# Self-attention in slots of one head: TensorE's instructions in a written order, and the causal mask added by VectorE

## The chip, the cores and the metric

The kernel runs on one core of a Trainium2 chip. The metric is the device time of one execution in microseconds (us). A core has TensorE (matrix products, PE in the profile, with its weight loads as PEld), VectorE (DVE), ScalarE (ACT), GpSimd (POOL) and SyncE (SP, which here issues transfers). They run side by side and wait for each other by semaphores. TensorE writes its results into PSUM[...]; everything else lies in SBUF.

## The reference

A decoder layer on x of shape (4, 512, 512) in fp32: self-attention, then a cross-attention to a context of (4, 512, 128), then a mixture of experts. Only the first part is touched:

```python
qkv = einsum('bsh,ph->bsp', layernorm(x), weight_qkv)   # 4 groups of 4 query heads, one key, one value head
scores = einsum('bsgqd,btgd->bgqst', q, k) / sqrt(128)
scores = where(causal, scores, finfo.min)
attn = softmax(scores, axis=-1)
out = einsum('bgqst,btgd->bsgqd', attn, v).reshape(b, s, 16 * 128)
x = x + einsum('bse,he->bsh', out, weight_proj)
```

There are four sequences (b) of 512 tokens, four groups (g) of four query heads (h), 64 heads in all, each of width 128.

## The kernel before

Tokens are cut into four tiles of 128 rows (s or i), and the 512 columns of x into four parts of 128 (c). For each sequence `norm_and_v` normalises x on VectorE and GpSimd (L143 to L151), turns it by transposes on TensorE into `xnT` (L171, copied out of PSUM by ScalarE) and computes the values `v` (`pv`, L220). For each group `project` computes the keys `kT`, and for each head the queries `qT` (`pq`, L236), each four products of 128x512 accumulated in one PSUM bank and copied out by ScalarE (L245, L248).

For each head, `softmax_rows` goes over the four row tiles i. Because of causality, tile i needs only the first (i+1)*128 columns of scores. It computes `sc` in PSUM (L258), and adds the mask of the diagonal block by a second product on TensorE, `ident16` times `mask16` in bf16, into the same bank (L265). VectorE takes the negated row maximum (L268), ScalarE the exponential with the row sum (L271), and VectorE divides (L279, L282). `attend` transposes the 10 blocks of the probabilities `pr` on TensorE (`tp`, L290), copies them to `prT` (L294; the copy for i = 1 by ScalarE, the others by VectorE), multiplies with `v` into `po` (L297), and ScalarE copies that to `oT` (L305). `add_projection` (L312, L319) multiplies the four `oT` of a group by `wpr`, and VectorE adds the result to x. For the last sequence these products (`pl` there) are done later, as filling in the cross-attention.

The softmax of a head is written ahead of `attend` of the head before it (`late`). No order is pinned in this part: the framework's scheduler takes the instructions by their priority and by its own estimate of what is ready, and fixes the order in which they stand on each engine. From the cross-attention on, the order is that of the program (`tc.keep_in_program_order`, through the wrapper `Ordered`).

PSUM is shared by tags with two banks each: `mm` (values, queries, keys, output products), `sc`, `t` (transposes) and `po`. `pr` has two buffers, `prT` one, `qT` three.

Of the kernel before, what the change touches and what calls it, by code (L numbers as in the profile page):

```python
# [35 lines left out]
def decoder_kernel(  # L36
# [23 lines left out]
    ident16 = const.tile([P, P], BF16, tag="ident16", name="ident16")  # L60
    nc.vector.tensor_copy(ident16, ident)
    maskf = const.tile([P, P], F32, tag="maskf", name="maskf")
    make_causal_mask(nc, maskf, mask_val=MASK)
    mask16 = const.tile([P, P], BF16, tag="mask16", name="mask16")
    nc.vector.tensor_copy(mask16, maskf)
# [68 lines left out]

    xb = [xpool.tile([P, NT, HID], F32, tag=f"x{b}", name=f"x{b}") for b in range(B)]
# [26 lines left out]
    def layernorm(b, dst):  # L162

        for part in norm_parts(b, dst, nc.vector, nc.gpsimd, nc.vector):
            part()

    def transpose_in(ps, src, dst, s, copy, bufs=2):

        t = ps.tile([P, NC, P], F32, tag="t", name="t", bufs=bufs)
        for c in range(NC):  # L170
            nc.tensor.transpose(t[:, c, :], src[:, c * P : (c + 1) * P], ident)  # L171
        copy(dst[:, :, s * P : (s + 1) * P], t)

# [5 lines left out]
    with ExitStack() as ph:  # L179
# [4 lines left out]
        nc.sync.dma_start(xb[0], x[0].rearrange("(s p) d -> p s d", p=P))  # L184
        wqkv_v = wqkvT.rearrange("(c p) (g w) -> p c g w", p=P, g=NKV)
        wv = wp.tile([P, NC, NKV, D], F32, tag="wv", name="wv")
        for c in range(NC):
            nc.sync.dma_start(wv[:, c], wqkv_v[:, c, :, (QPG + 1) * D :])
        wqk, wpr = [], []
        for g in range(NKV):  # L190
            t = wp.tile([P, NC, (QPG + 1) * D], F32, tag=f"wqk{g}", name=f"wqk{g}")
            nc.sync.dma_start(t, wqkv_v[:, :, g, : (QPG + 1) * D])
            wqk.append(t)
            t = pj.tile([P, QPG, HID], F32, tag=f"wpr{g}", name=f"wpr{g}")
            nc.sync.dma_start(
                t,
                wprojT[g * QPG * D : (g + 1) * QPG * D].rearrange(
                    "(h p) d -> p h d", p=P
                ),
            )  # L200
            wpr.append(t)
            if g + 1 < B:
                nc.sync.dma_start(
                    xb[g + 1], x[g + 1].rearrange("(s p) d -> p s d", p=P)
                )

        def norm_and_v(b):
            xnT = p2.tile([P, NC, S], F32, tag="xnT", name=f"xnT{b}", bufs=1)
            xn = [
                p2.tile([P, HID], F32, tag="xn", name=f"xn{b}_{s}", bufs=4)  # L210
                for s in range(NT)
            ]
            layernorm(b, lambda s: xn[s])
            for s in range(NT):
                transpose_in(ps, xn[s], xnT, s, nc.scalar.copy)
            v = []
            for s in range(NT):
                pv = ps.tile([P, HID], F32, tag="mm", name=f"pv{b}_{s}")
                for c in range(NC):
                    nc.tensor.matmul(  # L220
                        pv,
                        lhsT=xnT[:, c, s * P : (s + 1) * P],
                        rhs=wv[:, c].rearrange("p g d -> p (g d)"),
                        start=c == 0,
                        stop=c == NC - 1,
                    )
                vt = p2.tile([P, NKV, D], F32, tag="v", name=f"v{b}_{s}", bufs=5)
                nc.scalar.copy(vt.rearrange("p g d -> p (g d)"), pv)
                v.append(vt)
            return xnT, v  # L230

        def project(b, g, h, xnT):

            pq = ps.tile([P, S], F32, tag="mm", name=f"pq{b}_{g}_{h}")
            for c in range(NC):
                nc.tensor.matmul(  # L236
                    pq,
                    lhsT=wqk[g][:, c, h * D : (h + 1) * D],
                    rhs=xnT[:, c, :],
                    start=c == 0,  # L240
                    stop=c == NC - 1,
                )
            if h == QPG:
                t = p2.tile([P, S], F32, tag="kT", name=f"kT{b}_{g}")
                nc.scalar.copy(t, pq)  # L245
            else:
                t = p2.tile([P, S], F32, tag="qT", name=f"qT{b}_{g}_{h}", bufs=3)
                nc.scalar.mul(t, pq, QSCALE)  # L248
            return t

        def softmax_rows(b, g, h, qT, kT):
# [3 lines left out]
            for i in range(NT):  # L255
                n = (i + 1) * P
                sc = ps.tile([P, S], F32, tag="sc", name=f"sc{b}_{g}_{h}_{i}")
                nc.tensor.matmul(  # L258
                    sc[:, :n],
                    lhsT=qT[:, i * P : n],  # L260
                    rhs=kT[:, :n],
                    start=True,
                    stop=False,
                )
                nc.tensor.matmul(  # L265
                    sc[:, i * P : n], lhsT=ident16, rhs=mask16, start=False, stop=True
                )
                nc.vector.tensor_reduce(  # L268
                    nmx[:, i : i + 1], sc[:, :n], AX.X, ALU.max, negate=True
                )  # L270
                nc.scalar.activation(  # L271
                    pr[:, OFF[i] : OFF[i] + n],
                    sc[:, :n],
                    AF.Exp,
                    bias=nmx[:, i : i + 1],
                    accum_out=sm[:, i : i + 1],
                )
            rs = small.tile([P, NT], F32, tag="rs", name=f"rs{b}_{g}_{h}")
            nc.vector.reciprocal(rs, sm)  # L279
            for i in range(NT):  # L280
                q = pr[:, OFF[i] : OFF[i] + (i + 1) * P]
                nc.vector.tensor_scalar(q, q, rs[:, i : i + 1], None, ALU.mult)  # L282
            return pr

        def attend(b, g, h, pr, v):
            prT = p2.tile([P, NT, S], F32, tag="prT", name=f"prT{b}_{g}_{h}", bufs=1)
            for i in range(NT):
                t = ps.tile([P, NC, P], F32, tag="t", name=f"tp{b}_{g}_{h}_{i}")
                for j in range(i + 1):
                    nc.tensor.transpose(  # L290
# [4 lines left out]
            po = ps.tile([P, S], F32, tag="po", name=f"po{b}_{g}_{h}")  # L295
            for j in range(NT):
                nc.tensor.matmul(  # L297
                    po[:, j * P :],
                    lhsT=v[j][:, g, :],
                    rhs=prT[:, j, j * P :],  # L300
                    start=j == 0,
                    stop=j == NT - 1,
                )
            o = pj.tile([P, S], F32, tag="oT", name=f"oT{b}_{g}_{h}", bufs=NKV * QPG)
            nc.scalar.copy(o, po)  # L305
            return o

        def add_projection(b, g, outs):
            for s in range(NT):
                pj = ps.tile([P, HID], F32, tag="mm", name=f"pj{b}_{g}_{s}")  # L310
                for h in range(QPG):
                    nc.tensor.matmul(  # L312
                        pj,
                        lhsT=outs[h][:, s * P : (s + 1) * P],
                        rhs=wpr[g][:, h, :],
                        start=h == 0,
                        stop=h == QPG - 1,
                    )
                nc.vector.tensor_tensor(xb[b][:, s, :], pj, xb[b][:, s, :], ALU.add)  # L319

        late = None
        last_outs = []

        def finish(b, g, h, pr, v, outs):
            outs.append(attend(b, g, h, pr, v))
            if h == QPG - 1:
                if b == B - 1:
                    last_outs.append(outs)
                else:
                    add_projection(b, g, outs)  # L330

        for b in range(B):
            xnT, v = norm_and_v(b)
            for g in range(NKV):
                kT = project(b, g, QPG, xnT)
                outs = []
                for h in range(QPG):
                    qT = project(b, g, h, xnT)
                    pr = softmax_rows(b, g, h, qT, kT)
                    if late is not None:  # L340
                        finish(*late)
                    late = (b, g, h, pr, v, outs)
        finish(*late)


# [6 lines left out]


    pinned = False

    class Ordered:
        def __init__(self, engine):
            self.engine = engine

        def __getattr__(self, name):  # L360
            def call(*args, **kw):
                i = getattr(self.engine, name)(*args, **kw)  # L362
                if pinned:
                    tc.keep_in_program_order(i)
                return i

            return call

    tensor, vector, scalar, gpsimd, sync = (
        Ordered(e) for e in (nc.tensor, nc.vector, nc.scalar, nc.gpsimd, nc.sync)  # L370
    )
# [108 lines left out]
    with ExitStack() as ph:  # L480
# [415 lines left out]
        pinned = False  # L896
# [189 lines left out]
    with ExitStack() as ph:  # L1086
# [71 lines left out]
        pinned = True  # L1158
# [22 lines left out]
        pinned = False  # L1181
# [48 lines left out]
```

## Time and profile before

| | us |
|---|---|
| median of three runs | 2058.51 (2058.48 to 2058.69) |
| the profiled execution | 2059.55 |
| its span | 2057.7 |
| self-attention, to the first `pl` on TensorE | 908.91 |
| cross-attention and experts, the rest of the span | 1148.8 |

A row of a timeline gives the start and the length in us, the engine, the line, the operation, output<-input, and in brackets how long the engine had sat idle before it and for what. A row of a group gives the count, then the busy time in us and the mean of one in ns, then the idle time before them. A row of the busy time per stretch gives the stretch, its length, and for PE, PEld, DVE, ACT and POOL the busy us with the number of instructions in brackets, then the granted clock of TensorE, the share of the transfer engines and GB/s. An fp32 product stands in the profile as two passes (two rows), a transpose or a bf16 product as one. The recorded length of a pass is longer than the distance to the next one, as passes overlap.

### The profile page before, as it was taken

Reading aid. Unit: us, or ns where it says so; the run is one execution under the profiler, and the core shown is the slowest. Engines: PE = TensorE matmul, PEld = TensorE weight load, DVE = VectorE, ACT = ScalarE, POOL = GpSimd, SP = SyncE. Lnnn points to the kernel's source line nnn. Section 1 sums busy time; section 2 is a strip of 40 time slices with the busy share of each in tenths; the row PEclk is TensorE's granted clock in tenths of the full one; section 3 lists DMA queues with packets and bytes.
Section 4 is the critical chain, followed back from the end, with each engine's and each line's share of the span. In section 5 each row is a group of like instructions: output and inputs, shape, how many; then the busy total and the mean of one; then the engine's idle time right before and its main releaser. Section 6 shows DMA issues by size and latency. Waiting matters only on the chain. (4 is left out here: it accounts for less than half of the span.)

```text
span 2057.7 us, 22666 instructions
## 1 busy us (share of the span) xinstructions
PE 2020.7 (98%) x8507; PEld 946.0 (46%) x8507; DVE 867.4 (42%) x1843; ACT 680.0 (33%) x1479; POOL 197.8 (10%) x182
## 2 busy tenths in 40 slices
PE   7999999999999999999999999999999999999997
PEld 3555555554555545552233333333333354655664
DVE  4334344332444334435666656565656261111111
ACT  2322332222333224332555444444444201222221
POOL 1000000000000000010022020220200000233331
PEclk9999999999999999999999999999999999999999
DMA  8000000000000000000002300100010084333331
GB/s 286 0 1 0 1 0 0 1 0 0 1 0 1 0 1 0 1 25 19 17 14 51 86 12 17 52 13 12 21 49 6 1 286 136 76 62 59 67 56 22
DMA packets 52508, 74.80 MB, mean 36 GB/s; under 512 B 9889, under 2 KB 27809, under 8 KB 52402
## 3 DMA queue, kind: packets, MB, share of 16 engines
q1 hardware_dynamic: 43666, 54.73, 8.7%
q0 software_dynamic: 8736, 18.62, 5.0%
q8 instruction: 70, 1.15, 0.2%
q14 instruction: 36, 0.29, 0.0%
HBM read 47.60 MB, written 18.61 MB: 32 GB/s over the span
## 5 line engine op out<-in xcount | busy, mean ns | idle before, releaser
L362 DVE TENSOR_REDUCE cnmx<-s 128x1 f32<-128x512 f32 x512 | 329.2, 685 | 199.5 <-PE s L362 199.3
L362 ACT ACTIVATE w<-s 128x512 f32<-128x512 f32 x512 | 277.9, 594 | 338.9 <-PE s L362 338.8
L362 PE MATMUL s<-ckT,cqT 32*128 32x512 f32 x1024 | 308.8, 641 | 1.0 <-DVE cnmx L362 1.0
L236 PE MATMUL pq<-xnT,wqk 128*128 128x512 f32 x640 | 300.9, 593 | 0.0
L362 PE MATMUL s<-cqT,ckT 32*128 32x512 f32 x1024 | 294.8, 640 | 0.0
L268 DVE TENSOR_REDUCE nmx<-sc 128x1 f32<-128x128 f32 (+3 forms) x256 | 125.7, 491 | 185.0 <-PE sc L265 184.8
L271 ACT ACTIVATE pr<-sc,nmx 128x128 f32<-128x128 f32 (+3 forms) x256 | 135.1, 528 | 155.9 <-DVE nmx L268 155.9
L294 DVE COPY prT<-tp 128x128 f32<-128x128 f32 (+2 forms) x192 | 97.0, 507 | 206.4 <-PE tp L290 206.3
L258 PE MATMUL sc<-kT,qT 128*128 128x128 f32 (+3 forms) x512 | 181.3, 463 | 0.0
L312 PE MATMUL pj<-wpr,oT 128*128 128x512 f32 x384 | 171.8, 595 | 0.0
L362 PE MATMUL sh<-fnT,sw 128*128 128x512 f32 x320 | 154.0, 612 | 0.0
L297 PE MATMUL po<-prT,v 128*128 128x512 f32 (+3 forms) x512 | 149.4, 434 | 4.3 <-DVE prT L294 4.3
L236 PEld LDWEIGHTS pq<-xnT,wqk 128*128 128x128 f32 x640 | 110.6, 191 | 85.6 <-issue 85.5
L362 PEld LDWEIGHTS s<-cqT,ckT 32*128 32x128 f32 x1024 | 80.5, 183 | 145.3 <-ACT w L362 108.7
L362 PE MATMUL cpo<-w,vpad 128*32 128x512 f32 x1024 | 137.2, 608 | 0.0
L297 PEld LDWEIGHTS po<-prT,v 128*128 128x128 f32 x512 | 96.6, 190 | 84.5 <-issue 45.4
L248 ACT ACTIVATE qT<-pq 128x512 f32<-128x512 f32 x64 | 38.2, 597 | 225.0 <-PE pq L236 225.0
L362 PE MATMUL y<-w3all,hT 128*128 (+1 forms) x234 | 107.3, 594 | 3.1 <-ACT yo L1142 2.5
L258 PEld LDWEIGHTS sc<-kT,qT 128*128 128x128 f32 x512 | 81.4, 189 | 56.1 <-ACT qT L248 20.2
L312 PEld LDWEIGHTS pj<-wpr,oT 128*128 128x128 f32 x384 | 69.4, 190 | 77.4 <-issue 71.1
L290 PE MATMUL tp<-ident,pr 128*128 128x128 f32 x640 | 102.4, 275 | 1.3 <-DVE prT L294 1.3
L290 PEld LDWEIGHTS tp<-ident,pr 128*128 128x128 f32 x640 | 71.9, 141 | 62.6 <-issue 43.6
(162 smaller groups left out, 1948.7 us busy)
## 6 DMA issues: line engine op xcount, KB each, us to landing
w1all<-in_w1T SPq DMA_DIRECT2D x8, 704.0 KB
w2all<-in_w2T SPq DMA_DIRECT2D x8, 704.0 KB
wqk<-in_wqkvT SPq DMA_DIRECT2D x4, 1280.0 KB
x<-in_x SPq DMA_DIRECT2D x4, 1024.0 KB
wpr<-in_wprojT SPq DMA_DIRECT2D x4, 1024.0 KB
cqT<-cxnT SPq DMA_DIRECT2D x128, 32.0 KB
ckT<-ctxT SPq DMA_DIRECT2D x128, 32.0 KB
normed<-fxn SPq DMA_DIRECT2D x4, 1024.0 KB
```

The source lines that it names most:

```text
L236: nc.tensor.matmul(pq, lhsT=wqk[g][:, c, h * D : (h + 1) * D], rhs=xnT[:, c, :], start=c == 0, stop=c == NC - 1,)
L248: nc.scalar.mul(t, pq, QSCALE)
L258: nc.tensor.matmul(sc[:, :n], lhsT=qT[:, i * P : n], rhs=kT[:, :n], start=True, stop=False,)
L268: nc.vector.tensor_reduce(nmx[:, i : i + 1], sc[:, :n], AX.X, ALU.max, negate=True)
L271: nc.scalar.activation(pr[:, OFF[i] : OFF[i] + n], sc[:, :n], AF.Exp, bias=nmx[:, i : i + 1], accum_out=sm[:, i : i + 1],)
L290: nc.tensor.transpose(t[:, j, :], pr[:, OFF[i] + j * P : OFF[i] + (j + 1) * P], ident)
L294: copy(prT[:, : i + 1, i * P : (i + 1) * P], t[:, : i + 1, :])
L297: nc.tensor.matmul(po[:, j * P :], lhsT=v[j][:, g, :], rhs=prT[:, j, j * P :], start=j == 0, stop=j == NT - 1,)
L312: nc.tensor.matmul(pj, lhsT=outs[h][:, s * P : (s + 1) * P], rhs=wpr[g][:, h, :], start=h == 0, stop=h == QPG - 1,)
L362: i = getattr(self.engine, name)(*args, **kw)
```

## The change

The self-attention is rewritten as a list of small jobs that a loop puts in an order, and every TensorE instruction keeps that order. One turn of the loop is a slot. In it head u has its scores computed, and the head before it (`held`) its transposes and its product with the values.

- In the first half of a slot, scores 0 to 3 of head u, each followed by some projection jobs for the next head (`ahead`); in the second half, transposes 0 to 3 of the held head, each followed by jobs of `waiting`, that is output products of an earlier group or the first values; then the held head's `po`. The list `room` says how many jobs follow each step; a slot has 8 to 10 of them where there is enough waiting.
- The mask is no longer a product. VectorE adds `maskf` to the diagonal block in PSUM, ahead of its maximum. `ident16` and `mask16` go.
- At the end of a sequence the transposes of the next sequence's x stand between the scores of the last head; its values follow the last `po` of the old sequence in one block.
- The first sequence's x is loaded in four transfers in place of one, with moments, root and normalisation for each tile apart. The first group's `wqk` is issued ahead of `wv`.
- The other engines are not pinned in this part; the scheduler places their instructions around TensorE's order. In the experts' loop the pin is now for TensorE alone; only TensorE's calls go through the wrapper there in both kernels.

```diff
+    pinned_mm, pinned = True, False
...
+                if pinned or pinned_mm and self is tensor:
+                    tc.keep_in_program_order(i)
...
-        nc.sync.dma_start(xb[0], x[0].rearrange("(s p) d -> p s d", p=P))
+        for s in range(NT):
+            nc.sync.dma_start(xb[0][:, s, :], x[0, s * P : (s + 1) * P])
...
-        for c in range(NC):
-            nc.sync.dma_start(wv[:, c], wqkv_v[:, c, :, (QPG + 1) * D :])
         wqk, wpr = [], []
         for g in range(NKV):
...
             nc.sync.dma_start(t, wqkv_v[:, :, g, : (QPG + 1) * D])
             wqk.append(t)
+            if g == 0:
+                for c in range(NC):
+                    nc.sync.dma_start(wv[:, c], wqkv_v[:, c, :, (QPG + 1) * D :])
...
+        def norm_first():
...
+            for s in range(NT):
...
+                nc.vector.bn_stats(st, xb[0][:, s, :])
+                nc.vector.bn_aggr(mv, st)
...
+                nc.vector.tensor_scalar(rstd, mv[:, 1:2], EPS, None, ALU.add)
+                nc.gpsimd.tensor_tensor(rstd, rstd, mhalf[:, 0:1], ALU.pow)
+                nc.vector.tensor_scalar(
+                    xn, xb[0][:, s, :], mv[:, 0:1], rstd, ALU.subtract, ALU.mult
+                )
...
+        def product(name, operands, done):
+            held = []
+
+            def job(k, lhsT, rhs):
+                if k == 0:
+                    held.append(ps.tile([P, S], F32, tag="mm", name=name))
+                tensor.matmul(
+                    held[0], lhsT=lhsT, rhs=rhs, start=k == 0, stop=k == len(operands) - 1
+                )
+                if k == len(operands) - 1:
+                    done(held[0])
+
+            return [lambda k=k, o=o: job(k, *o) for k, o in enumerate(operands)]
...
+            def part(i):
                 n = (i + 1) * P
                 sc = ps.tile([P, S], F32, tag="sc", name=f"sc{b}_{g}_{h}_{i}")
-                nc.tensor.matmul(
...
-                nc.tensor.matmul(
-                    sc[:, i * P : n], lhsT=ident16, rhs=mask16, start=False, stop=True
-                )
+                tensor.matmul(
+                    sc[:, :n], lhsT=qT[:, i * P : n], rhs=kT[:, :n], start=True, stop=True
+                )
+                nc.vector.tensor_tensor(
+                    sc[:, i * P : n], sc[:, i * P : n], maskf, ALU.add
+                )
                 nc.vector.tensor_reduce(
...
+            def divide():
+                rs = small.tile([P, NT], F32, tag="rs", name=f"rs{b}_{g}_{h}")
+                nc.vector.reciprocal(rs, sm)
+                for j in range(NT):
+                    w = pr[:, OFF[j] : OFF[j] + (j + 1) * P]
+                    nc.vector.tensor_scalar(w, w, rs[:, j : j + 1], None, ALU.mult)
...
+        waiting, ahead, held = values(0), [], None
+        for u in units + [None]:
+            between, turns = [lambda: None] * NT, []
+            take = 4
+            if u is not None:
+                b, g, h = u
+                pr, between, divide = scores(u)
+                if (b, g) == (0, 0):
+                    take = 8 if h < 2 else 0
                 else:
...
+                    take = (4, 5, 5, 2)[h]
+                if (g, h) == (NKV - 1, 1) and b + 1 < B:
+                    norm(b + 1)
+                if h + 1 < QPG:
+                    ahead = project(b, g, h + 1)
+                elif g + 1 < NKV:
+                    ahead = project(b, g + 1, QPG) + project(b, g + 1, 0)
+                elif b + 1 < B:
+                    turns = [lambda s=s: turn(b + 1, s) for s in range(NT)]
+
+            room = [1, 1, 1, 1, 1, 1, 0, 2] if held else [1, 1, 1, 1, 0, 0, 0, 0]
+            total = min(take, len(waiting)) + len(ahead) + (8 if turns else 0)
+            for k in (1, 2, 0, 3, 7, 5, 4) * 2:
+                room[k] += sum(room) < total
+            for k in (5, 4, 0, 3, 2, 1) * 2:
+                room[k] -= sum(room) > total and room[k] > 0
+            steps = attend(*held) if held else []
+            for k in range(2 * NT):
+                if k < NT:
+                    between[k]()
+                    if turns:
+                        turns.pop(0)()
+                        if not turns:
+                            ahead = project(b + 1, 0, QPG) + project(b + 1, 0, 0)
+                elif steps:
+                    steps.pop(0)()
+                for _ in range(room[k]):
+                    some = ahead or waiting
+                    if some:
+                        some.pop(0)()
+            for job in ahead:
+                job()
+            ahead = []
+            for step in steps:
+                step()
+            if u is not None:
+                divide()
+            if held:
+                b_, g_, h_ = held[0]
+                if h_ == QPG - 1 and b_ < B - 1:
+                    waiting += output(b_, g_)
+                if h_ == QPG - 1 and g_ == NKV - 1 and b_ < B - 1:
+                    for job in values(b_ + 1):
+                        job()
+            held = (u, pr) if u is not None else None
```

`values`, `project` and `output` make their jobs with `product`; `attend` gives the four transpose steps and the step of `po`, with the same instructions as before.

## The prediction

> **What bounds the kernel now.** First the page. TensorE is busy for 98% of the span, the next engine for 42%:
>
> ```profile
> PE 2020.7 (98%) x8507; PEld 946.0 (46%) x8507; DVE 867.4 (42%) x1843; ACT 680.0 (33%) x1479; POOL 197.8 (10%) x182
> ```
>
> A busy TensorE need not run at its pace, so the stretch of the self-attention comes next, then its timeline. By the view of busy time per stretch, of the first 905 us:
>
> ```profile
> 0.00:905.00 905.00, 886.52 (x3128) 472.20 (x3128) 361.65 (x878) 278.93 (x752) 15.64 (x38) 1.00 0.05 18
> ```
>
> VectorE is busy for 40% and ScalarE for 31%: neither bounds the stage. The granted clock is 1.00. The order of the two built programs is the same, instruction for instruction, from the last head to the end, so only these 905 us can change. One head on TensorE:
>
> ```profile
> 312.24 0.38 PE L258 MATMUL sc<-kT,qT 128*128 128x128 f32 x2
> 312.46 0.22 PE L265 MATMUL sc<-mask,ident 128*128 128x128 bf16 x1
> 312.51 0.65 PE L258 MATMUL sc<-kT,qT 128*128 128x256 f32 x2
> ...
> 315.30 0.22 PE L265 MATMUL sc<-mask,ident 128*128 128x128 bf16 x1
> 315.36 0.50 PE L290 MATMUL tp<-ident,pr 128*128 128x128 f32 x3
> 315.69 1.88 PE L312 MATMUL pj<-wpr,oT 128*128 128x512 f32 x4
> 317.41 2.32 PE L297 MATMUL po<-prT,v 128*128 128x512 f32 x8
> 319.56 2.39 PE L312 MATMUL pj<-wpr,oT 128*128 128x512 f32 x5
> ```
>
> Read the starts, not the durations. Four passes of 512 columns take 317.41 - 315.69 = 1.72 us, 0.429 each (an fp32 matmul is two passes, a transpose one); the eight passes of `po` 2.15 us; a transpose 0.109 (three in 0.33). The scores have the shapes of `po`, so their floor is 2.15 too. But 312.24 to 315.69 is 3.45 us, and its scores and seven transposes are worth 2.15 + 0.76 = 2.91: 0.54 us a head goes to the masks. Of this 4 x 0.056 = 0.22 is their own time; the rest is in score passes that start late behind a mask, or behind the exp that frees their bank.
>
> The floor without masks: 640 `pq`, 384 `pj` and 128 `pv` passes at 0.429 = 494.2; 64 `po` and 64 score sets at 2.15 = 275.2; 704 transposes at 0.109 = 76.7; together 846.1 us. The masks add 256 x 0.056 = 14.3. The stage ends here:
>
> ```profile
> 905.82 2.42 PE L297 MATMUL po<-prT,v 128*128 128x512 f32 x8 [0.78 <-DVE prT L294]
> 908.91 1.55 PE L362 MATMUL pl<-wpr,oT 128*128 128x512 f32 x3 [0.68 <-ACT oT L305]
> ```
>
> 908.9 - 860.4 = 48.5 us are lost: 14.1 at the start (below), 64 x 0.32 = 20.5 around the masks, some 14 at batch changes and in the last heads.
>
> **The change part by part: the masks.** Their removal gives 14.3 + 20.5 = 34.8 us, if no other wait takes the same place. [...] The trace decides: passes follow at 0.429 us with a load of 0.19 us each hidden. A load is exposed only behind something as short as a mask, and a transpose (0.109) just covers one. I keep 34.8.
>
> VectorE gets 256 adds on PSUM. No row shows VectorE writing PSUM. Nearest rows:
>
> ```profile
> L319 DVE TENSOR_TENSOR x<-pj,x 128x512 f32<-128x512 f32 x48 | 33.2, 691 | 111.6 <-PE pj L312 111.6
> L294 DVE COPY prT<-tp 128x128 f32<-128x128 f32 x64 | 18.6, 291 | 203.8 <-PE tp L290 203.7
> ```
>
> Bounds: 0.19 us (the 128-wide cast that goes away) and 0.69 (the 512-wide sum); I take 0.29. [...] 256 x 0.29 = 74 us of VectorE against 14 of TensorE. [...] With 361.65 us busy it goes to 436 of some 890, 49%. So the add costs nothing by its sum; its place in the chain counts.
>
> **The chain in a slot.** TensorE now may not pass a waiting instruction. A slot is: scores 0 to 3 of head u with projection jobs between them (a job is two passes, 0.858 us), the transposes of head u-1 with jobs between, then `po` of u-1. By the order view VectorE does, after score 3: add, maximum, first prT copy, reciprocal, four divides, two prT copies; `po` waits for the last copy. Durations:
>
> ```profile
> 315.56 0.69 DVE L268 TENSOR_REDUCE nmx<-sc 128x1 f32<-128x512 f32 x1 [0.44 <-PE sc L265]
> 316.28 0.69 ACT L271 ACTIVATE pr<-sc,nmx 128x512 f32<-128x512 f32 x1 [0.46 <-DVE nmx L268]
> 316.87 0.19 ACT L271 ACTIVATION_READ_ACCUMULATOR pr<-sc,nmx 128x1 f32 x1
> 317.09 0.18 DVE L279 RECIPROCAL rs<-sm 128x4 f32<-128x4 f32 x1 [0.25 <-ACT pr L271]
> 317.31 1.27 DVE L282 TENSOR_SCALAR pr<-pr,rs 128x128 f32<-128x128 f32 x4
> ```
>
> From the end of score 3: 0.20 until VectorE sees it (315.36 to 315.56), add 0.29, step 0.04, maximum 0.69, exp and sum 0.81, reciprocal and divides 1.52, copies 0.47 + 0.68 (of 128x384 and 128x512, the first 0.55 by its row, 0.08 of it under its neighbour), load and start of `po` 0.15: 4.8 us. TensorE gets there after five jobs and ten transposes, 4.29 + 1.09 = 5.38. Slack 0.55, so no wait in the 30 full slots of this form; in 12 (h = 2) an x sum of 0.61 stands ahead of the copies: slack nil. Exposed waits, by kind of slot:
> - h = 3, nine slots: the eight jobs run k, then q. An output product is open in one of the two `mm` banks, so q's first job waits until ScalarE has copied kT: 0.20 + 0.59 + load 0.15 = 0.95. 8.6 us.
> - Thin slots (four jobs; group 0 and most of the last batch), ten. Exp 0 ends 0.22 + 0.20 + 0.29 + 0.04 + 0.29 + 0.03 + 0.46 = 1.53 us into the slot, with a load 1.68; score 2 is there at 0.22 + 0.43 + 0.86 = 1.51: 0.18. Transposes 2 need the first copy's bank: behind the add, 0.49 + 0.29 + 0.16 = 0.94 after score 3, and TensorE is there at 0.33: 0.61. The copies stand ahead of the divides here, so `po` does not wait. 7.9 us.
> - Three last slots of a batch: kT waits 0.95 for the fourth xnT copy, q 0.95 for kT: 5.7. Three first slots: score 2 0.18, transposes 2 (first copy behind the maximum, 1.66 against 1.18) 0.48, transposes 3 (the copy on ScalarE behind exp 3, 2.56 against 1.99) 0.57: 3.7.
> - Last head and drain, nothing between: score 2 (1.69 against 0.65) 1.04, score 3 0.19, transposes 2 0.61, `po` for the copies of transposes 3 1.04; then 0.43, 1.04, and `pl` for oT (0.20 + 0.59 + load) 0.94: 5.3.
>
> **The start.**
>
> ```profile
> 6.51 1.29 DVE L143 BATCH_NORM_STATS2 st<-x 128x6 f32<-128x512 f32 x2 [6.51 <-DMA x<-in_x]
> ...
> 11.58 2.91 PE L171 MATMUL t<-ident,xn 128*128 128x128 f32 x12 [11.58 <-DVE xn L151]
> ...
> 16.71 13.04 PE L220 MATMUL pv<-wv,xnT 128*128 128x512 f32 x30
> ...
> 29.59 0.59 PE L236 MATMUL pq<-xnT,wqk 128*128 128x512 f32 x1
> ```
>
> By 29.59 TensorE did 32 x 0.429 + 16 x 0.109 = 15.5 us: 14.1 lost. Now x[0] comes in quarters. At 391 GB/s (the rate of 10 to 40 us) 1.05 MB took until 6.51, so quarters land at some 4.5, 5.2, 5.8 and 6.5 (bounds 4.5 and 6.5 for all; the last one counts). The last moments are done at 7.4; SP's three further issues of 0.44 delay what follows by 1.3, under the transfer. GpSimd's four powers (1.0 each in place of one) end at 9.2, the last xn at 9.7, its transposes and copy at 11.3; kT starts at 11.6, 9.85 lost. wqk0 (1.31 MB more, now ahead of wv) is in at 9.9. Then sc0 waits 0.95 for qT, and sc2 0.8, since VectorE has the norm of x[1] (landing 18.8, moments 2.9, power 1.0, a multiply) queued ahead of the first add. 11.6 us in all. The two casts that go (0.19, 0.22) were hidden behind the moments. Moved projections and transposes are the same instructions, at their floor.
>
> **The sum.** Lost after: 11.6 + 8.6 + 7.9 + 5.7 + 3.7 + 5.3 = 42.8, and 1 for small bubbles as in the trace. The first `pl` comes at 846.1 + 43.8 = 889.9 in place of 908.9: 19 us sooner. The profiled execution took 2059.55 us (span 2057.7, 1.85 around it), 1.04 above the median of 2058.51; from the median, 2039.5.
>
> **The rivals.**
> *The order feeds TensorE better than I count* (kT's copy and the thin slots' waits hidden): only start and end are lost, 846.1 + 16.9 = 863, 46 us sooner: 2012.6. Against it: the bank that q needs is plainly held.
> *The wait at `po` takes the masks' place* (slower). If the chain is longer than 4.8 by d, the 12 slots lose d and the 30 lose d - 0.55. At d = 0.85 the gain is gone; at 0.95 it is slower by over 0.2%; at 1.2, 34 us lost, 2073.5. For it: a read behind a PSUM write on one engine is in no row, and an add of 0.69 is 0.40 by itself. Against: VectorE's step from reciprocal to divide is 0.04.
> *The start and the small waits eat it.* If VectorE's norms in the first slots wait on late loads (5 us) and each wait above is half again as long (16 us), 2058: no difference.
> That the order is not what the diff says is ruled out by the order view.
>
> **How the numbers follow.** My forecast (waits as counted, within some 12 us) 0.75, 2040; better feeding 0.09; `po` waits 0.11, of which 0.02 within 0.2% and 0.08 slower; start and small waits 0.05, mostly no difference. 0.2%, 4.1 us, is about what a measurement can tell. Faster 0.86, same 0.06, slower 0.08. The add at 0.69 costs 12 x 0.4 = 5 us, at 0.19 gains nothing; the start's bounds 2 us either way; the range goes from 2025, where half of the 26 us of waits in the slots are hidden, to 2055, where `po` waits as with d = 0.75.
>
> **What would show it.** The first `pl` near 890 us; no row of masks; score passes of 384 and 512 columns at 0.322 and 0.429; an L336 add at 0.29; `po` with little wait for prT; q's load waiting for kT nine times near 0.9. Wrong if `po` waits over 0.3 us in most slots, if an add takes over 0.6, or if the start is not 2 us earlier.

## The result, and the profile after

The changed kernel takes 2042.55 us (median of four runs, 2040.03 to 2043.65); the kernel before, run beside it, 2058.59. The ratio is 0.992, with a 95% interval of 0.9903 to 0.9938: faster by 0.8%. The profiled execution took 2043.63 us, its span 2041.7.

First the page's line of engines, then the view of busy time per stretch up to the end of the self-attention, then the group of the new add (columns: busy us, mean ns of one, then the idle time ahead of it):

```profile
PE 1996.7 (98%) x8251; PEld 934.3 (46%) x8251; DVE 936.0 (46%) x2100; ACT 681.0 (33%) x1479; POOL 199.0 (10%) x185
```

```profile
0.00:890.00 890.00, 862.26 (x2882) 460.36 (x2883) 431.75 (x1139) 280.51 (x753) 17.07 (x41) 1.00 0.05 18
```

```profile
L336 DVE TENSOR_TENSOR sc<-sc,maskf 128x128 f32<-128x128 f32 x256 | 76.6, 299 | 371.6 <-PE sc L141 371.5
```

TensorE is still busy for 98% of the span and has 256 products fewer. VectorE took the masks at 0.299 us each and is busy for 431.75 of the first 890 us. Neither number says where the 19 us are; the timeline does. One full slot (batch 1, group 1, head 1) on TensorE:

```profile
316.73 1.02 PE L141 MATMUL sc<-kT,qT 128*128 128x512 f32 x2
317.58 1.02 PE L141 MATMUL pj<-wpr,oT 128*128 128x512 f32 x2
318.44 0.27 PE L141 MATMUL tp<-ident,pr 128*128 128x128 f32 x1
318.55 1.02 PE L141 MATMUL pj<-wpr,oT 128*128 128x512 f32 x2
319.41 0.38 PE L141 MATMUL tp<-ident,pr 128*128 128x128 f32 x2
319.63 1.02 PE L141 MATMUL pj<-wpr,oT 128*128 128x512 f32 x2
320.49 0.93 PE L141 MATMUL tp<-ident,pr 128*128 128x128 f32 x7
321.25 1.88 PE L141 MATMUL pj<-wpr,oT 128*128 128x512 f32 x4
322.97 2.32 PE L141 MATMUL po<-prT,v 128*128 128x512 f32 x8
```

Every start follows the one above at its floor: score 3's two passes 0.85, a job 0.86, a transpose 0.11. From score 3's end at 317.58 to `po` at 322.97 TensorE needs 5.39 us. VectorE's chain in the same stretch has to fit into that:

```profile
317.78 0.30 DVE L336 TENSOR_TENSOR sc<-sc,maskf 128x128 f32<-128x128 f32 x1 [0.83 <-PE sc L141]
318.12 0.69 DVE L339 TENSOR_REDUCE nmx<-sc 128x1 f32<-128x512 f32 x1
318.75 0.29 DVE L371 COPY prT<-tp 128x128 f32<-128x128 f32 x1
319.65 0.18 DVE L352 RECIPROCAL rs<-sm 128x4 f32<-128x4 f32 x1 [0.61 <-ACT pr L342]
319.87 1.28 DVE L355 TENSOR_SCALAR pr<-pr,rs 128x128 f32<-128x128 f32 x4
321.06 1.15 DVE L371 COPY prT<-tp 128x384 f32<-128x384 f32 x2
```

The last copy ends at 322.21, 4.63 us after score 3; with the 0.15 that the prediction counts for load and start that is 4.78, inside 5.39. So `po` does not wait. What does wait is named by the view of waits and by the group of the projections (mean ns, then the idle time and its releasers):

```profile
PEld pq L141 <- ACT kT L295: 18.0, 12, 1.5
```

```profile
L141 PE MATMUL pq<-xnT,wqk 128*128 128x512 f32 x640 | 317.1, 595 | 10.8 <-ACT kT L295 8.1 <-ACT xnT L250 2.7
```

Twelve times q stands behind kT's copy: each time 0.84 us lie between the starts beyond the floor, and another 0.10 in the passes behind. Start and end of the stage, by the timeline:

```profile
8.89 3.40 PE L141 MATMUL xt<-ident,xn 128*128 128x128 f32 x16 [8.89 <-DVE xn L238]
12.96 7.13 PE L141 MATMUL pq<-xnT,wqk 128*128 128x512 f32 x16 [0.68 <-ACT xnT L250]
20.78 0.49 PE L141 MATMUL sc<-kT,qT 128*128 128x128 f32 x2 [0.69 <-ACT qT L299]
...
886.32 2.42 PE L141 MATMUL po<-prT,v 128*128 128x512 f32 x8 [0.79 <-DVE prT L371]
889.42 1.13 PE L141 MATMUL pl<-wpr,oT 128*128 128x512 f32 x2 [0.68 <-ACT oT L384]
```

The first `pl` comes at 889.42 in place of 908.91: 19.5 us sooner. The span is 16.0 us shorter. The 3.5 us between come later, where the two programs are the same, and the last section has them.

### The profile page after: what moved, and what is told of

It reads as the page before. It is cut to its first block, busy times and chain, and to the rows that moved or that the text cites. A ratio compares the mean times of both kernels' runs of the same rounds, so it can differ in the third digit from the quotient of the medians.

```text
span 2041.7 us, 22321 instructions
## 1 busy us (share of the span) xinstructions
PE 1996.7 (98%) x8251; PEld 934.3 (46%) x8251; DVE 936.0 (46%) x2100; ACT 681.0 (33%) x1479; POOL 199.0 (10%) x185
## 5 line engine op out<-in xcount | busy, mean ns | idle before, releaser
L141 PE MATMUL pq<-xnT,wqk 128*128 128x512 f32 x640 | 317.1, 595 | 10.8 <-ACT kT L295 8.1
L336 DVE TENSOR_TENSOR sc<-sc,maskf 128x128 f32<-128x128 f32 x256 | 76.6, 299 | 371.6 <-PE sc L141 371.5
L141 PE MATMUL pj<-wpr,oT 128*128 128x512 f32 x384 | 187.3, 593 | 0.0
L141 PEld LDWEIGHTS sc<-kT,qT 128*128 128x128 f32 x512 | 89.2, 190 | 92.9 <-issue 78.7
L384 ACT COPY oT<-po 128x512 f32<-128x512 f32 x64 | 37.5, 586 | 244.3 <-PE po L141 244.3
L141 PEld LDWEIGHTS tp<-ident,pr 128*128 128x128 f32 x640 | 78.3, 141 | 79.6 <-issue 36.6
L141 PE MATMUL h<-w1all,xT 128*128 x312 | 98.7, 459 | 0.9 <-issue 0.9
```

The source lines that it names most:

```text
L336: nc.vector.tensor_tensor(sc[:, i * P : n], sc[:, i * P : n], maskf, ALU.add)
```

## The experiments

Each kernel is compared by its time and by the start of its first `pl`, which leaves out what happens in the rest of the program.

**e1: the mask as a product again, in the new order.**

```diff
-                    ... rhs=kT[:, :n], start=True, stop=True
+                    ... rhs=kT[:, :n], start=True, stop=False
-                nc.vector.tensor_tensor(sc[:, i * P : n], sc[:, i * P : n], maskf, ALU.add)
+                tensor.matmul(sc[:, i * P : n], lhsT=ident16, rhs=mask16, start=False, stop=True)
```

(The tiles of the first moments share tags with the later ones, to make room for the two bf16 tiles.)

> The changed kernel with the mask put back as a TensorE product (bf16 identity x bf16 mask) right behind each score product; slots, order, input quarters stay. Theory (a mask costs TensorE its own 0.056 us and about as much again, because the next load is not covered by so short a pass): 256 x 0.11 = 28 us, less some 4 us of the small waits that the 0.30 us add had made: first pl at 889.4 + 24 = 913, about 2067 us. Rival A (only the product's own time counts, the rest of the loss was the scheduler's order): + 14, less 4: first pl at 899, about 2052. Rival B (the mask was worth nothing, the written order brought all): first pl within 3 us of 889.4, about 2043.

Measured: 2071.83 us (2069.72 to 2073.39), 1.006 of the kernel before (1.0043 to 1.0077); first `pl` at 920.32. The written order without the moved mask is slower than the kernel before. The timeline shows the price of one mask:

```profile
329.11 1.02 PE L145 MATMUL sc<-kT,qT 128*128 128x512 f32 x2
329.97 0.22 PE L145 MATMUL sc<-mask,ident 128*128 128x128 bf16 x1
330.02 1.08 PE L145 MATMUL pj<-wpr,oT 128*128 128x512 f32 x2
330.94 0.27 PE L145 MATMUL tp<-ident,pr 128*128 128x128 f32 x1
```

The mask takes 0.056 us from its start to that of `pj`, and the two passes of `pj` behind it take 0.92 us and not 0.86: 0.056 more, in the second of them. In the trace the weights of this second pass begin to load 0.056 us behind the start of the first (in the kernel before, behind the mask at 40.76 us, by as much), where elsewhere they mostly begin within 0.003 us of it; that so short a product doesn't cover the load before them, which takes 0.19 us, is argued from this. Full slots are 0.44 us longer, four times 0.11. Of the 30.9 us by which the first `pl` is later, 2.8 lie ahead of the first score (2.0 of them because the first projections began at half clock, 9.15 us in place of 7.13, as the last section explains) and 28.1 in the slots: the 28 of the theory. Its deduction of 4 us for smaller waits did not come: the thin slots lose 0.48, no less than the others. Both rivals fall.

**e2: the kernel before, only the mask moved.**

```diff
-                    stop=False,
+                    stop=True,
-                nc.tensor.matmul(sc[:, i * P : n], lhsT=ident16, rhs=mask16, start=False, stop=True)
+                nc.vector.tensor_tensor(sc[:, i * P : n], sc[:, i * P : n], maskf, ALU.add)
```

> The kernel before with one edit: the mask added by VectorE on the score tile; start, slots and the order of TensorE left to the scheduler as before. Theory (34.8 us hang on the masks, but some of them on the exp that frees a score bank, which stays): per head the loss falls from 0.54 to about 0.27 us, so 64 x 0.27 = 17 us sooner: first pl near 892, about 2041 us: the mask alone brings nearly what the whole change does, and what the order gains at the start it gives back in its waits. Rival A (all of the masks' loss goes): first pl near 874, about 2024. Rival B (without the written order the freed time turns into waits for the add): less than 5 us sooner, about 2054.

Measured: 2043.43 us (2038.96 to 2044.84), ratio 0.9916 (0.9899 to 0.9932); first `pl` at 892.14, 16.8 us sooner than before. The one edit brings what the whole change brings. What stays lost is another thing: 57 times score 2 of a head follows a transpose some 0.18 us late, together 10.3 us, and each time its load had waited for the exp that frees the bank. The group of the score's loads names the exp and the q copy:

```profile
L254 PEld LDWEIGHTS sc<-kT,qT 128*128 128x128 f32 x512 | 81.2, 189 | 77.1 <-ACT pr L267 32.7 <-issue 23.7 <-ACT qT L244 19.9
```

Waits of this size between a transpose and a score are not in the kernel before (0.05 us each there, 3.0 together): with the masks gone, they took a part of their place.

What the order is worth follows less surely. With the product kept (e1) it costs 11.4 us against the kernel before. With the mask moved, the first `pl` of the changed kernel is 2.7 us ahead of e2's, but TensorE's clock alone can make that difference. In the profile of e2 it is at half from 887.19 to 890.60, under the last `po`:

```profile
887.54 3.93 PE L293 MATMUL po<-prT,v 128*128 128x512 f32 x8 [0.81 <-DVE prT L290]
892.14 4.13 PE L358 MATMUL pl<-wpr,oT 128*128 128x512 f32 x9 [0.68 <-ACT oT L301]
```

From this `po` to `pl` it is 4.60 us, against 3.10 in the changed kernel; and the changed kernel's start had a whole clock early, which was worth some 2.1 us (last section). The medians are no further apart than the runs of one kernel, and of the executions with a granted clock of 0.999, e2's took 2038.96 us and the changed kernel's 2040.03. So the written order with these banks removes the score waits and pays with q's, and no gain of it over the moved mask alone is shown.

**e3: a third bank for the projections.**

```diff
-                    held.append(ps.tile([P, S], F32, tag="mm", name=name))
+                    held.append(ps.tile([P, S], F32, tag="mm", name=name, bufs=3))
-                po = ps.tile([P, S], F32, tag="po", name=f"po{b}_{g}_{h}")
+                po = ps.tile([P, S], F32, tag="po", name=f"po{b}_{g}_{h}", bufs=1)
```

> The changed kernel with PSUM banks dealt anew: three for mm in place of two, one for po in place of two. Theory (q's first job waits 0.84 us for kT's copy only because an output product holds the other mm bank, 12 times): 10 us sooner, first pl near 879.4, about 2033 us, and the waits of pq for kT gone. Rival A (kT itself is needed at once, or the copy's time shows elsewhere: the first score of the next head waits for kT or qT instead): first pl within 3 us of 889.4. Rival B (one po bank makes po wait for the oT copy of the head before): first pl later than 889.4, a row of po waiting for oT.

Measured: 2029.18 us (2028.53 to 2031.02), ratio 0.9856 (0.984 to 0.9873), faster than the changed kernel too, whose interval ends at 0.9903. First `pl` at 879.47. In the group of the projections kT is gone as a releaser:

```profile
L141 PE MATMUL pq<-xnT,wqk 128*128 128x512 f32 x640 | 316.1, 597 | 2.7 <-ACT xnT L250 2.7
```

The twelve slots are 0.94 us shorter each, 11.3 together, and all other slots between the first and the last keep their length to 0.01. (The start gives back 1.5, since TensorE's first projections run at half the clock there; the last section has it.) One bank for `po` costs nothing in these slots; in the changed kernel the oT copy ends 1.77 us or more before the next `po` starts.

**e4: three further adds per score.**

```diff
-                nc.vector.tensor_tensor(sc[...], sc[...], maskf, ALU.add)
+                for m in (maskf,) + (none,) * 3:
+                    nc.vector.tensor_tensor(sc[...], sc[...], m, ALU.add)
```

(`none` is a constant tile of zeros; the moments' tags are shared as in e1.)

> The changed kernel with three further adds of a tile of zeros (128x128, VectorE, on the same score columns) behind each mask add: the chain from score 3 to po grows by 3 x 0.30 = 0.90 us and VectorE by 256 x 0.9 = 230 us. It tests the slack that the sum gave to po: measured in the changed kernel, the last prT copy ends 0.77 (h=1), 0.70 (h=3), 0.48 (h=0) and 0.17 us (h=2) before po starts, 0.15 of each the load. Theory (the slack is all that hides the add): h=2 slots lose 0.9 each, h=1 and h=3 about 0.3, h=0 about 0.6, thin slots and slots at batch ends about 1.8 each: 12 x 0.9 + 18 x 0.3 + 12 x 0.6 + 20 x 1.8 = 60 us later, first pl near 949, about 2100 us; a wait of po for prT appears. Rival (VectorE is at half load, so nothing is lost but in the thin slots): + 20 to 36 us at most, no po wait in full slots, about 2070.

Measured: 2077.8 us (2074.93 to 2080.15), ratio 1.0093 (1.0077 to 1.011); first `pl` at 925.40, 36.0 us later and not 60. The full slots of h = 1, 2 and 3 lose nothing, because VectorE's order is another one: the scheduler now puts the divides behind the last two copies, so the copies don't wait for them, and `po` still starts 0.44 to 0.80 us after the last copy. The thin slots lose 1.5 to 1.9 each, mostly at score 2, which waits for the exp that frees its bank:

```profile
L143 PE MATMUL sc<-kT,qT 128*128 128x128 f32 (+3 forms) x512 | 182.0, 442 | 28.9 <-ACT pr L345 28.2
```

So this run did not test the slack at `po`, and neither theory is borne out: the rival's 20 to 36 us hold its sum, but 9.5 of them fall into the last slot, for reasons that neither named (e9).

**e5: the last two copies twice.**

```diff
-                copy(prT[:, : i + 1, i * P : (i + 1) * P], t[:, : i + 1, :])
+                for _ in range(2 if i > 1 else 1):
+                    copy(prT[:, : i + 1, i * P : (i + 1) * P], t[:, : i + 1, :])
```

> The changed kernel with each of VectorE's two last prT copies of a head (128x384 and 128x512) issued twice, so the last one ends 0.55 + 0.69 - 0.08 = 1.16 us later; VectorE's order is otherwise that of the changed kernel, divides ahead of the copies. e4 did not test the slack at po, because the divides were placed behind the copies there. Theory (slack at po, beyond the load of 0.15, as measured in the changed kernel: 0.62 us for h=1, 0.55 for h=3, 0.33 for h=0, 0.02 for h=2; what exceeds it is lost): 12 x 1.14 for h=2, and 30 x 0.65 for the others on the mean = 33 us: first pl near 922, about 2076 us, and po waits for prT in 42 slots: the rival of the prediction then has its place and its price right, and the chain was only short enough. Rival (VectorE has time and catches up, TensorE loses nothing): first pl within 5 us of 889.4.

Measured: 2092.27 us (2091.82 to 2093.26), ratio 1.016 (1.0143 to 1.0177); first `pl` at 940.50. Now `po` waits, as in this h = 1 slot by the timeline:

```profile
321.60 1.88 PE L141 MATMUL pj<-wpr,oT 128*128 128x512 f32 x4
323.95 2.42 PE L141 MATMUL po<-prT,v 128*128 128x512 f32 x8 [0.47 <-DVE prT L372]
```

VectorE's copies in the same slot:

```profile
321.69 2.21 DVE L372 COPY prT<-tp 128x384 f32<-128x384 f32 x4
```

The last one ends at 323.90, and `po` starts 0.05 us behind it.

Lengths of slots, from the first score of a head to that of the next, less those of the changed kernel, in us:

| slots | changed kernel | e1 | e3 | e4 | e5: expected | e5: measured |
|---|---|---|---|---|---|---|
| h = 1, full (12) | 13.14 | +0.44 | 0.00 | 0.00 | +0.54 | +0.46 |
| h = 2, full (12) | 13.14 | +0.44 | 0.00 | 0.00 | +1.14 | +1.05 |
| h = 3, full (9) | 14.94 | +0.69 | -0.94 | 0.00 | +0.61 | +0.52 |
| h = 0, full (9) | 12.28 | +0.44 | 0.00 | +0.48 | +0.83 | +0.74 |
| thin (10) | 9.50 | +0.48 | 0.00 | +1.51 to +1.89 | | +0.42 |
| last head to `pl` | 13.81 | +0.03 | 0.00 | +9.47 | | +11.89 |

The 42 full slots lose 12 x 0.46 + 12 x 1.05 + 9 x 0.52 + 9 x 0.74 = 29.5 us (expected 33): the slack at `po` is real, and 1.16 us more in the chain makes the kernel slower than before. The other 21.6 us are the thin and odd slots 7.4, the start 2.3, and the last slot 11.9, of which the longer chain explains some 2.4 (the rest under e9).

**e6: the third bank without the written order.** The score, mask and all else as in e2:

```diff
-            pq = ps.tile([P, S], F32, tag="mm", name=f"pq{b}_{g}_{h}")
+            pq = ps.tile([P, S], F32, tag="mm", name=f"pq{b}_{g}_{h}", bufs=3)
```

(and so for `pv` and `pj`, with `bufs=1` for `po`.)

> e2 (the kernel before, mask added by VectorE, order of TensorE left to the scheduler) with the banks of e3: three for mm, one for po. Theory (a second mm bank was missing only in the written order, where k and q follow one another while an output product is open; e2's trace has no pq wait at all, its losses are score passes that wait for the exp): no gain, first pl within 2 us of 892.1, about 2043 us; so the written order with three banks (e3, 879.5) is what beats the scheduler. Rival (a third bank lets any order feed TensorE better): first pl near 882, about 2033.

Measured: 2044.14 us (2041.89 to 2044.64), ratio 0.9924 (0.9907 to 0.994); first `pl` at 891.97 beside e2's 892.14. No gain: the bank helps only the order that lacked it. The written order pays with its third bank: e3 takes 2029.18 us beside 2044.14 here, with the first `pl` 12.5 us sooner, some 1.4 of them because the clock is at half under the last `po` here as in e2.

**e7: e3 with x[0] in one transfer.**

```diff
-        for s in range(NT):
-            nc.sync.dma_start(xb[0][:, s, :], x[0, s * P : (s + 1) * P])
+        nc.sync.dma_start(xb[0], x[0].rearrange("(s p) d -> p s d", p=P))
```

> e3 with x[0] again in one transfer of 1.05 MB (the rest of the start as in e3, wqk ahead of wv). Theory (quarters let VectorE start on the moments at 3.5 us in place of 6.5): the first transposes start near 9.7 us in place of 7.9, k near 14 in place of 12.3, first pl about 1.7 us later, 881.2; no difference that the time can show. Rival (the last quarter decides, it lands no sooner than the whole): k starts within 0.4 us of 12.3.

Measured: 2030.65 us (2028.39 to 2032.41), ratio 0.9858 (0.9842 to 0.9874), no difference in the time from e3. The trace sees it: transposes at 10.30, k at 14.74 (e3: 7.89, 12.32), first `pl` at 881.70, 2.2 us later. The quarters bring 2.2 us.

**e8: e3 with the first prT copy on ScalarE.**

```diff
-                copy = nc.scalar.copy if i == 1 else nc.vector.tensor_copy
+                copy = nc.scalar.copy if i < 2 else nc.vector.tensor_copy
```

> e3 with the first prT copy of a head (128x128) on ScalarE as well as the second, so that it no longer stands behind the add and the maximum of score 3 on VectorE. Theory: the 18 waits of transposes 2 and 3 for a bank (7.3 us in e3) shrink by 0.2 to 0.3 us each, 4 us; first pl near 875.5, about 2025 us. Rival (ScalarE's copies stand ahead of exp 3 there, and what is saved at the transposes comes back as a wait of po in the h=2 slots): first pl within 1.5 us of 879.5 or later.

Measured: 2033.39 us (2030.86 to 2033.43), ratio 0.9875 (0.9858 to 0.9891); first `pl` at 881.55. Thin slots are 0.06 shorter (expected 0.2 to 0.3), full h = 2 slots 0.12 longer, and the last one 0.50 longer: the rival is right, and e3 stays the best version.

**e9: e5 with the next stage's fills on VectorE.**

```diff
-        gpsimd.memset(rows0, 0.0)
+        vector.memset(rows0, 0.0)
```

(and so for the thirteen others.)

> e5 with the fourteen constant fills of the next stage's tiles (two rows, cqT, ckT, vpad) on VectorE in place of GpSimd. In e4 and e5 the last slot grew by 9.5 and 11.9 us beyond what the longer chain explains, and the four divides of head (3,3,2) took 6.23 and 7.57 us in place of 1.27 while GpSimd's fills ran. Theory (the fills hold VectorE up where its operation goes from SBUF to SBUF): those divides take 1.3 us again; the fills now stand in VectorE's own queue, at 0.2 to 0.5 us each and six of them ahead of the last head's scores, so the last slot gets back 6.3 less 1.2 to 3: first pl near 936. Rival (the divides are held up by something else, such as the doubled copies or the transfers): they take over 5 us again, first pl near 940.5 or later.

Measured: first `pl` at 931.97, 8.5 us sooner than e5 and 4 sooner than expected; one run, 2080.89 us. The four divides of head (3,3,2) by the timeline, in e5:

```profile
912.60 7.57 DVE L355 TENSOR_SCALAR pr<-pr,rs 128x128 f32<-128x128 f32 x4
```

and in e9, with one of the fills ahead of them:

```profile
911.52 0.48 DVE L141 MEMSET rows<- 4x512 f32 x1
911.94 1.13 DVE L355 TENSOR_SCALAR pr<-pr,rs 128x128 f32<-128x128 f32 x4
```

The fills on GpSimd were what held the divides. On VectorE each fill of 128x512 takes 0.48 us. The last slot's surplus falls from 11.89 to 4.45, but not by the fills alone. What they cost TensorE shows in the time from the last head's first score to its score 2: 1.60 us in the changed kernel, 6.45 in e5, 1.89 in e9. Another part is TensorE's clock, which was at half in four windows of 3.4 us in the last slot of e5 and in one in that of e9 (last section). In e5 the scores 2 and 3, the first `po` and the way from the last `po` to `pl` fall into such windows and take 1.4, 1.5 and 1.7 us longer than in the changed kernel, some 4.6 in all; in e9 one `po` does, 1.6 longer. In e4 three such windows run from 905.86 to 916.10.

## Why the prediction was right, step by step

Lost on TensorE against the floor of 846.1 us, in us. Measured is the distance from each pass's start to the next one's, less the floor of its shape, added up by kind of slot:

| step | predicted | measured |
|---|---|---|
| the start | 11.6 | 12.18 |
| h = 3: q behind kT's copy, nine | 8.6 | 8.75 |
| thin slots, ten | 7.9 | 6.80 |
| last slots of a batch, three | 5.7 | 5.77 |
| first slots of a batch, three | 3.7 | 3.33 |
| last head and drain | 5.3 | 5.18 |
| small bubbles | 1.0 | 1.30 |
| sum | 43.8 | 43.31 |
| first `pl` | 889.9 | 889.4 |

*The masks.* Their removal was put at 34.8 us: 14.3 of their own and 20.5 around them. e1 puts the products themselves at 28.1 in the written order, and e2 finds 16.8 in the scheduler's order (18.3 had its last `po` had a whole clock). Of the 20.5, then, about 14 stand behind a mask in the written order too. In e2 10.3 us come back as scores that wait, which is the prediction's own condition ("if no other wait takes the same place") failing there; the written order keeps them off.

*The loads.* The prediction read from the trace that the loads of long passes are hidden and that a transpose just covers one. e1 bears that out: long passes keep 0.429 us beside loads of 0.19 us, and two of them take 0.86 us behind a transpose (from 331.05 to 331.91 us) but 0.92 behind a mask. What is lost there is 0.056 us, not a whole load.

*The add.* 0.29 was taken, 0.299 measured. 128 columns take 0.299 us where the sum of 512 takes 0.691, so by these two some 0.17 us of each add does not depend on its width (an estimate). Moving the masks cost 76.6 us of VectorE and nothing on TensorE's path in the full slots, whose bubbles are 1.30 us in all. VectorE's load was not the limit either: in e4 it is busy for 197 us more (1133.5 in place of 936.0), and the full slots of h = 1 to 3 lose nothing.

*The chain to* `po`. 4.8 against 5.38 was predicted (the terms add up to 4.85), 4.78 against 5.39 measured at h = 1. The slack isn't one number of 0.55 for 30 slots: with the 0.15 that the prediction counts for load and start, it is 0.62, 0.55 and 0.33 for h = 1, 3 and 0, and 0.02 for h = 2, where "nil" was said. That term was too large: a `po` that waits starts 0.05 us behind the copy (e5), so each slack is 0.10 more. The 1.16 us of e5 less 0.72, 0.12, 0.65 and 0.43 makes 0.44, 1.04, 0.51 and 0.73 for h = 1, 2, 3 and 0, the measured losses to 0.02.

*The rival at* `po`. e5 gives it its place and its price: with d = 1.16 the prediction's rule makes 12 x 1.16 + 30 x 0.61 = 32 us, and 29.5 were measured in the full slots. Longer adds alone would not have brought it about: in e4 they make the scheduler order VectorE differently, and the loss comes at score 2 of the thin slots.

*The start.* The sum is right to 0.6 us by errors that cancel and by luck. The last quarter lets its moments start at 7.28, later than the whole transfer did (6.51). GpSimd's powers take 0.56 to 0.76 us and not 1.0, but VectorE put all the moments ahead of the first xn, and the sixteen transposes, most of them at half clock, took 3.40 us, so k starts at 12.96 and not 11.6. Score 2 of the first slot, said to wait 0.8, doesn't. e7 puts the quarters at 2.2 us. The luck is TensorE's clock, which the prediction left out: it was whole at 11.77 us in this profile, and at 16.3 to 18.6 in six of the other seven with this order. With the projections as slow as in e3, the first `pl` would have come near 891.5 (an estimate, 889.4 and 2.1).

*From the first* `pl` *to the end* nothing was predicted to change, and this is the one term that was off: 1148.8 us before, 1152.3 after, with the same instructions in the same order. This is most of why the median is 2042.55 and not 2040: the one execution with a granted clock of 0.999 took 2040.03. The last section shows where it lies.

## What to carry to other kernels

The mask product between long passes cost TensorE about twice its own time here (0.11 us for 0.056, e1), so the mask added by a half-idle VectorE paid, though it takes that engine five times as long as the product (0.299 us). A written order should be looked through for two products of one pool that follow each other while a third is open: dealing the banks anew took 11.3 us off the slots here, where the order alone had brought nothing over the moved mask that these runs can tell from the clock. A slack is worth measuring slot by slot, since the sum may hold where a single slot has none left. And before a difference of a few us between two profiles is put down to an edit, the granted clock of both belongs beside it.

## What the runs showed of the hardware that was not expected

**TensorE's clock at half, in windows of 3.4 us, some with little or no idle time ahead of them.** The view of stretches of the changed kernel (after the engines' busy times: granted clock, DMA share, GB/s):

```profile
1083.00:1086.90 3.90, 3.90 (x30) 1.39 (x29) 3.28 (x7) 1.69 (x4) 0.00 (x0) 1.00 0.04 8
1086.90:1090.30 3.40, 3.06 (x12) 0.88 (x7) 2.53 (x6) 2.17 (x4) 0.72 (x1) 1.00 0.00 0
1090.40:1093.80 3.40, 3.40 (x18) 0.93 (x19) 2.50 (x7) 0.00 (x0) 0.00 (x0) 0.50 0.00 0
1093.80:1097.20 3.40, 3.40 (x24) 0.91 (x16) 2.82 (x7) 2.17 (x4) 0.00 (x0) 1.00 0.12 21
...
1636.50:1639.90 3.40, 3.40 (x11) 2.41 (x11) 0.26 (x2) 0.00 (x0) 0.00 (x0) 0.50 1.03 368
1639.90:1643.30 3.40, 3.40 (x5) 1.34 (x4) 2.87 (x11) 0.23 (x1) 0.00 (x0) 0.50 0.89 321
```

The first window is 3.4 us long and the second 6.8, which counts as two: three in all, and in the kernel before one, at 1340.9. Each costs what is done at half pace in it, some 1.6 us. Counted over all profiled runs, the time from the first `pl` to the end follows their number (the last 7 to 10 us, where every kernel has half the clock, are left out of the count):

| half-clock windows after the first `pl` | kernels | us from the first `pl` to the end |
|---|---|---|
| 0 | e3, e4, e8, e9 | 1147.2 to 1147.8 |
| 1 | before, e1, e7 | 1148.8 to 1149.6 |
| 2 | e2, e5, e6 | 1150.8 to 1150.9 |
| 3 | after | 1152.3 |

So the 3.5 us are two windows more, and they belong to the execution rather than to the change: e3, e8 and e9 have the changed order and none, and the four executions of the changed kernel had a granted clock of 0.996, 0.996, 0.997 and 0.999 and took 2043.63, 2043.65, 2041.46 and 2040.03 us.

The end of the self-attention, ahead of the first `pl`, has such windows too: one in e2, e6 and e9, three in e4 and four in e5, none in the others. There each window, or the first of a row, follows a stretch of 3.4 us in which TensorE was busy for less than 2 us. In e5:

```profile
922.20:925.60 3.40, 3.40 (x9) 1.60 (x8) 1.81 (x5) 0.93 (x3) 0.00 (x0) 0.50 0.00 0
925.60:929.00 3.40, 1.55 (x9) 0.98 (x8) 3.16 (x9) 0.89 (x3) 0.00 (x0) 1.00 0.00 0
929.00:932.40 3.40, 3.40 (x9) 2.16 (x8) 0.61 (x2) 0.14 (x1) 0.00 (x0) 0.50 0.00 0
932.40:935.80 3.40, 1.44 (x11) 0.88 (x9) 2.54 (x5) 0.76 (x2) 0.00 (x0) 1.00 0.00 0
935.80:939.20 3.40, 3.40 (x5) 1.69 (x6) 0.00 (x0) 0.00 (x0) 0.00 (x0) 0.50 0.00 0
```

The busy time is 1.55 and 1.44 us ahead of the last two windows; in the same place of the changed kernel it is 2.36 and more, and the clock stayed whole. Single idle gaps need not be long: the longest ahead of the last two of e5 is 1.85 us, and ahead of the window at 1090 TensorE was busy for 3.06 of the 3.40 us, though with products of 32 rows, often one at a time. What sets a window off was not tried and stays open. The same clock moves the start: the sixteen first projections take 7.13 us in the changed kernel and 9.27 in e3, whose clock becomes whole only at 16.6 us.

**GpSimd's fills hold up VectorE's divides.** In e5 the four divides stretch over 7.57 us in place of 1.27 while GpSimd fills tiles from 912.45 to 920.26; the first alone lasts 5.54, through eleven fills in a row. With the fills on VectorE (e9) they take 1.13. By what the one engine holds up the other no run shows. VectorE's operations that read PSUM ran on beside the fills: in the changed kernel the fills run from 873.68 to 881.21, and four adds between them take 0.29 to 0.30 us each, as elsewhere. There the divides end at 874.05, 0.37 us into the first fill, which takes 0.82 us where the next takes 0.51, and the next divides start at 881.58, behind the last. That the changed kernel and e3 pay nothing for these fills is a matter of 1 us: with 0.90 us (e4) and 1.16 us (e5) more in each chain, the divides took 6.23 and 7.57 us.
